# Three regroupings in a two-layer transformer kernel: the start's order, the last groups' output products, and where the quantiser runs

## The chip, the cores and the metric

The kernel runs on one core of one Trainium2 chip. Its time is the device time of one execution in microseconds (us), and the figure compared is the median over several executions. Below, the engines have the names of the profile: PE is the tensor engine (matrix products), DVE the vector engine, ACT the scalar engine, POOL the GpSimd engine, and SP the engine whose queue issues most of the DMA transfers. ACT also issues a few. Each engine works off its own instructions strictly in order.

## The reference

Input is x, 8 sequences of 512 tokens with 256 channels, in float32. Two layers follow each other, each of the form x + attention(norm(x)) + feed(norm(x)).

```python
xn = layernorm(x)
# layer 0
q, k, v = (xn @ W + b for W, b in ((Wq, bq), (Wk, bk), (Wv, bv)))   # 16 heads of 64
q, k = rope(q), rope(k)
p = softmax(where(causal, q @ k.T / sqrt(64), -1e9))
attention = (p @ v) @ Wo + bo
x_scale = max(abs(xn).max() / 127, 1e-5)          # over all 8 sequences
x_int8 = clip(round(xn / x_scale), -128, 127)
feed = (x_int8 @ weight_int8.T) * x_scale * weight_scale + bias
x = x + attention + feed
# layer 1
xn = layernorm(x)
comparison = (xn @ compare_left) @ (xn @ compare_right).T / sqrt(256)
attention = (comparison > threshold) * softmax(comparison + gate_bias) @ xn
prev = xn shifted down by one token, zeros first
r = sigmoid((mu_r * xn + (1 - mu_r) * prev) @ W_r.T)
k = square(relu((mu_k * xn + (1 - mu_k) * prev) @ W_k.T))
feed = r * (k @ W_v.T)
return x + attention + feed
```

## The kernel before

**Order.** Both layers are written under a manual schedule: the order of the calls in the source is the order of the instructions on every engine. Each call below (scores, soften, divide, ...) issues to one or several engines, so the place of a call decides what it stands behind on each of them. PSUM is eight banks of 128x512 float32, all of one pool (`bank`, L60); a bank comes free when its last reader has read it, and a product that finds no free bank waits.

**Layer 0** works in 16 groups `at`: sequence b = at // 2, and half g of its heads (8 heads). For each group:

- `project_qk` (L352), for half a group and for queries (0) or keys (1): eight products on PE (L363), two copies with bias on ACT into a buffer l (L368), and four DMAs on SP's queue that write l with its quarters swapped into y (L370). l and y have two buffers each. `turn_qk` (L373) applies the rotation: two products on DVE (L378), into h and in place in y, and the add h + y on POOL (L381).
- `project_v` (L384): products (L392), copies on ACT (L398), and a store to DRAM; `load_v` reads it back in another layout as vr.
- `scores(at, run)` (L418), in five runs, each with one or two pairs of banks sc (L429). `soften` (L436): DVE adds the mask and takes row minima (L452), ACT takes the exponential (L456) with its sum. `divide` (L462): reciprocals on DVE (L467), scaling on POOL (L472). `turn` (L480): transposes on DVE (L492).
- `weigh` (L497): 256 small products on PE (L505) into four banks av, when all five runs are turned. `keep_weighed` (L513): ACT copies them into four tiles att (L519).
- `finish` (L331), one group later: 16 products pw per half of the tokens with wo on PE (L340) and the sum with x1 on DVE (L344); after a sequence's second group x1 is stored to DRAM.

Around these: `look_at` and `prepare` normalise an input, `transpose_x` transposes it on PE, stores the transposed one in DRAM as xnf and keeps its greatest magnitude. When the last has been seen, `scale_of_x` makes the quantiser's scale xs. `quantise(b, r, xq)` (L177) then takes the tile read back from xnf (128x1024, float32, xnl) in three steps on POOL to whole numbers kept in bf16:

```python
nc.gpsimd.tensor_scalar(r, r, xs[:, 1:2], ROUND, ALU.mult, ALU.add)      # L181
nc.gpsimd.tensor_scalar(xq_, r, -ROUND, -128.0, ALU.add, ALU.max)        # L182
nc.gpsimd.tensor_scalar(xq_, xq_, 127.0, 127.0, ALU.min, ALU.min)        # L183
```

`add_quantised` (L185) multiplies xq with the int8 weights held in bf16 (PE, L191), scales on DVE (L196) and adds to x1 on POOL (L199). Sequences 0 and 1 are done inside groups 12 and 13, between `project(at + 1, 0)` and `scores(at, 2)`; sequences 2 to 7 in layer 1.

The head of the layer (L530 to L562), where the pipeline fills, and its tail (L647 to L682, groups 14 and 15) are written out by hand. Weights come by `load_group(which, g, n)`: which is 0 for q, 1 for k, 2 for v, and a quarter g is one tile of 4 heads. `load_rest` and `load_second` issue wo and other constants on ACT's queue.

**Layer 1** is one loop over b (L829 to L856): `compare` (c L727, row maxima L731, exponentials L740, threshold L743), `key` (pk L755, relu on ACT L759, square on POOL L760), `turn_input(b + 1)` (pyt L215), `gate` (pg L770, sigmoid L774), `sides_of(b + 1)` (plr L226), `mix` (ACT L706, DVE L710), `value` twice (pvv L782, product on DVE L786, sum on POOL L787), `turn_chances` (trc L795, copies ptc on ACT L797 and DVE L799), `complete` (the quantised part of sequence b + 2), `end` twice (po L808, y L814, store), `norm(b + 2)`, and `fetch_late(b + 3)`, which fetches x1 and xnf of that sequence and quantises it.

Of the kernel before, what the change touches and what calls it, by code (L numbers as in the profile page):

```python
# [16 lines left out]
P = 128  # L17
# [27 lines left out]
def two_layers(  # L45
# [131 lines left out]
    def quantise(b, r, xq):  # L177

        r = r.rearrange("p a n -> p (a n)")
        xq_ = xq.rearrange("p k n -> p (k n)")  # L180
        nc.gpsimd.tensor_scalar(r, r, xs[:, 1:2], ROUND, ALU.mult, ALU.add)  # L181
        nc.gpsimd.tensor_scalar(xq_, r, -ROUND, -128.0, ALU.add, ALU.max)  # L182
        nc.gpsimd.tensor_scalar(xq_, xq_, 127.0, 127.0, ALU.min, ALU.min)  # L183
# [57 lines left out]
    with ExitStack() as c0:  # L241
# [9 lines left out]
        away = pool("away", 2, space=bass.MemoryType.DRAM)  # L251

# [70 lines left out]
        def fetch(b):  # L323
            x1s[b] = output_tile(f"x1_{b}")
            nc.sync.dma_start(x1s[b], tokens(b))
# [5 lines left out]
        def finish(at):  # L331

            b, g = divmod(at, NH)
            for half in range(2):
                rows = slice(2 * half, 2 * half + 2)
                pw = bank(f"pw_{at}_{half}").rearrange("p (j n) -> p j n", j=2)
                for j in range(2):
                    tok = bass.ts(2 * half + j, P)
                    for p in range(4):
                        nc.tensor.matmul(  # L340
                            pw[:, j, :], atts[at, p][:, tok], wo[:, 4 * g + p, :],
                            start=(p == 0), stop=(p == 3),
                        )
                nc.vector.tensor_tensor(x1s[b][:, rows, :], pw, x1s[b][:, rows, :], ALU.add)  # L344
            if g == NH - 1:
                nc.sync.dma_start(x1_far[b], x1s[b].rearrange("p t n -> p (t n)"))

# [165 lines left out]
        def keep_weighed(at):  # L513
            g = at % NH
            for j, av in enumerate(weighed.pop(at)):
                atts[at, j] = attp.tile([P, S], F32, tag="att", name=f"att_{at}_{j}")
# [16 lines left out]
        project_qk(0, 0)  # L533
        project_qk(0, 1)
        turn_qk(0, 0)
        project_qk(1, 0)
        turn_qk(0, 1)
        x_next.append(load_x(1))
        project_qk(1, 1)
        for which in (1, 0, 2):  # L540
            load_group(which, 2, 2)
        turn_qk(1, 0)
        project_v(0)
        turn_qk(1, 1)
# [12 lines left out]
        turn_qk(2, 0)  # L557
        project_qk(3, 0)
        scores(0, 1)
# [3 lines left out]
        for at in range(last):  # L563
# [67 lines left out]
            soften(at, 4)  # L631
            turn(at, 3)
            if two:
# [10 lines left out]
            elif at == last - 1:  # L644
                nc.sync.dma_start(w2, second.rearrange("j (k p) n -> p j k n", p=P))
# [28 lines left out]
        finish(at - 1)  # L674
# [10 lines left out]
    with ExitStack() as c1:  # L685
# [7 lines left out]
        def fetch_late(b):  # L693
            fetch_output(b, act.tile([P, NT, D], F32, tag="x1", name=f"x1l_{b}", bufs=4))
            xq = act.tile([P, NK, S], BF16, tag="xq", name=f"xq_{b}")
            quantise(b, fetch_input(b, act.tile([P, NK, S], F32, tag="xnl", name=f"xnl_{b}")), xq)
            return xq
# [130 lines left out]
        xq = fetch_late(2)  # L828
        for b in range(B):  # L829
            compare(b)  # L830
            kk = key(b)
            if b + 1 < B:
# [19 lines left out]
            if b + 3 < B:  # L852
                xq = fetch_late(b + 3)
# [69 lines left out]
```

## Time and profile before

| quantity | value |
|---|---|
| times of 3 runs | 991.24, 994.87, 997.51 us; median 994.87 |
| profiled execution, its own time | 990.11 us |
| span of the profile | 988.0 us |
| mean granted PE clock in it | 0.986 of full |
| PE busy | 942.1 us, 95% |
| DVE busy | 777.1 us, 79% |
| POOL busy | 599.5 us, 61% |
| ACT busy | 530.2 us, 54% |
| DMA | 106.45 MB, mean 108 GB/s |

The span is the time between the first and the last recorded instruction; the execution's own time is 2.1 us longer. A row of a group list reads: line, engine, operation, output<-input with sizes, number of instructions, then busy us and mean ns of one, then the engine's idle time just before these instructions and what ended it. A row of a timeline reads: start in us, duration in us, engine, line, operation, and in brackets the idle time before it with its releaser. "issue" as releaser means that the profile shows nothing that was waited for. A q after an engine's name (ACTq) is its queue of DMA issues.

### The profile page before, as it was taken

Reading aid. Unit: us, or ns where it says so; the run is one execution under the profiler, and the core shown is the slowest. Engines: PE = TensorE matmul, PEld = TensorE weight load, DVE = VectorE, ACT = ScalarE, POOL = GpSimd, SP = SyncE. Lnnn points to the kernel's source line nnn. Section 1 sums busy time; section 2 is a strip of 40 time slices with the busy share of each in tenths; the row PEclk is TensorE's granted clock in tenths of the full one; section 3 lists DMA queues with packets and bytes.
Section 4 is the critical chain, followed back from the end, with each engine's and each line's share of the span. In section 5 each row is a group of like instructions: output and inputs, shape, how many; then the busy total and the mean of one; then the engine's idle time right before and its main releaser. Section 6 shows DMA issues by size and latency. Waiting matters only on the chain.

```text
span 988.0 us, 27412 instructions
## 1 busy us (share of the span) xinstructions
PE 942.1 (95%) x10491; PEld 599.9 (61%) x10491; DVE 777.1 (79%) x2417; ACT 530.2 (54%) x1480; POOL 599.5 (61%) x710
## 2 busy tenths in 40 slices
PE   9898999999999999999999999999797799999998
PEld 5345565655657565656566565656376576667776
DVE  4597988898899889887988997889876477677764
ACT  3365565656564755655575647474653534445553
POOL 3396665656575666666555758897644356566621
PEclk9899999999999999999999999999898999999999
DMA  6784354525452553445255445443530212221110
GB/s 186 198 238 108 87 123 138 127 70 132 143 127 69 132 143 91 109 150 117 78 130 150 123 116 130 132 127 73 132 88 13 75 64 75 76 75 52 45 32 33
DMA packets 61219, 106.45 MB, mean 108 GB/s; under 512 B 7585, under 2 KB 38305, under 8 KB 61089
## 3 DMA queue, kind: packets, MB, share of 16 engines
q1 hardware_dynamic: 59216, 103.06, 38.4%
q8 instruction: 83, 1.36, 0.6%
q10 hardware_dynamic: 1872, 1.64, 0.5%
q14 instruction: 48, 0.39, 0.1%
HBM read 39.66 MB, written 29.36 MB: 70 GB/s over the span
## 4 chain that ended last, share of the span: by engine, by line
PE 80%; POOL 8%; DVE 4%; issue 4%; DMA 3%; ACT 1%; SPq 0%; DVEq 0%; ACTq 0%; POOLq 0%
PE pq L363 21%; PE av L505 13%; PE sc L429 13%; PE pw L340 11%; PE pv L392 10%; PE po L808 3%; PE pvv L782 3%; POOL xq L182 2%; POOL xq L183 2%; PE trc L795 1%; POOL kk L760 1%; DMA xnl<-xnf 1%; DVE p L452 1%; PE pk L755 1%; PE acc L191 1%
## 5 line engine op out<-in xcount | busy, mean ns | idle before, releaser
L456 ACT ACTIVATE p<-p,nm 128x64 f32<-128x64 f32 (+15 forms) x512 | 260.0, 511 | 152.9 <-DVE nm L452 122.3
L472 POOL TENSOR_SCALAR p<-p,rs 128x64 f32<-128x64 f32 (+15 forms) x512 | 264.6, 542 | 55.0 <-DVE rs L467 53.6
L381 POOL TENSOR_TENSOR h<-h,y 128x1024 f32<-128x1024 f32 x64 | 167.8, 2622 | 189.2 <-DVE y L378 100.6
L452 DVE CUSTOM_DVE_ANT_0 p<-sc,cmask 128x64 f32<-128x64 f32 (+15 forms) x512 | 191.0, 436 | 77.1 <-PE sc L429 76.6
L492 DVE STREAM_TRANSPOSE t<-p 128x256 f32<-128x256 f32 (+3 forms) x640 | 193.5, 368 | 22.3 <-POOL p L472 20.0
L429 PE MATMUL sc<-h,h 64*32 64x512 f32 (+15 forms) x4096 | 145.9, 397 | 7.6 <-POOL h L381 6.0
L505 PE MATMUL av<-t,vr 32*64 32x96 f32 (+15 forms) x4096 | 131.6, 400 | 13.4 <-issue 13.4
L505 PEld LDWEIGHTS av<-t,vr 32*64 32x64 f32 x4096 | 126.2, 133 | 18.7 <-issue 15.8
L429 PEld LDWEIGHTS sc<-h,h 64*32 64x32 f32 x4096 | 76.9, 106 | 93.2 <-issue 66.9
L363 PE MATMUL pq<-xnT,wk 128*128 128x512 f32 x256 | 116.9, 609 | 6.1 <-DMA wk<-in_Wk 4.6
L368 ACT ACTIVATE l<-pq,cs 128x512 f32<-128x512 f32 x128 | 84.4, 682 | 67.5 <-PE pq L363 58.2
L378 DVE TENSOR_TENSOR y<-y,cs 128x1024 f32<-128x1024 f32 x64 | 109.4, 1710 | 8.7 <-DMA y<-l 8.7
L340 PE MATMUL pw<-wo,att 128*128 128x256 f32 x512 | 114.5, 381 | 0.7 <-ACT att L519 0.7
L363 PE MATMUL pq<-xnT,wq 128*128 128x512 f32 x256 | 114.4, 598 | 0.2 <-ACT xnT L299 0.2
L392 PE MATMUL pv<-wv,xnT 128*128 128x512 f32 x256 | 114.0, 598 | 0.0
L340 PEld LDWEIGHTS pw<-wo,att 128*128 128x128 f32 x512 | 95.7, 190 | 16.6 <-issue 2.1
L456 ACT ACTIVATION_READ_ACCUMULATOR p<-p,nm 128x1 f32 x512 | 96.9, 189 | 0.0
L363 PEld LDWEIGHTS pq<-xnT,wk 128*128 128x128 f32 x256 | 48.3, 194 | 67.9 <-issue 63.7
L392 PEld LDWEIGHTS pv<-wv,xnT 128*128 128x128 f32 x256 | 47.4, 190 | 57.7 <-issue 54.2
L519 ACT ACTIVATE att<-av,cs 128x512 f32<-128x512 f32 x64 | 38.9, 688 | 80.8 <-PE av L505 80.8
L378 DVE TENSOR_TENSOR h<-l,cs 128x1024 f32<-128x1024 f32 x64 | 78.8, 1231 | 4.3 <-ACT l L368 4.3
L363 PEld LDWEIGHTS pq<-xnT,wq 128*128 128x128 f32 x256 | 47.4, 190 | 56.6 <-issue 48.3
(95 smaller groups left out, 1005.9 us busy)
## 6 DMA issues: line engine op xcount, KB each, us to landing
y<-l SPq DMA_DIRECT2D x256, 128.0 KB, 2.3
va<-v SPq DMA_DIRECT2D x32, 512.0 KB, 3.0
vr<-va SPq DMA_DIRECT2D x64, 256.0 KB, 4.6
x<-in_x SPq DMA_DIRECT2D x15, 512.0 KB, 4.4
xnf<-xnT SPq DMA_DIRECT2D x8, 512.0 KB, 3.9
x1f<-x SPq DMA_DIRECT2D x8, 512.0 KB, 2.8
xnl<-xnf SPq DMA_DIRECT2D x8, 512.0 KB, 5.0
out<-y SPq DMA_DIRECT2D x14, 256.0 KB, 2.7
```

The costliest lines, as they stand in the source:

```text
L340: nc.tensor.matmul(pw[:, j, :], atts[at, p][:, tok], wo[:, 4 * g + p, :], start=(p == 0), stop=(p == 3),)
L363: nc.tensor.matmul(pb, w[:, g, k, bass.ts(t, P)], xnT[b][:, k, :], start=(k == 0), stop=(k == NK - 1),)
L368: nc.scalar.activation(l[:, t, :], pb, AF.Identity, bias=cs[:, bias : bias + 1])
L378: nc.vector.tensor_tensor(dst, src, table[:, None, :].to_broadcast([P, 2, S]), ALU.mult)
L381: nc.gpsimd.tensor_tensor(h, h, y, ALU.add)
L392: nc.tensor.matmul(pb.rearrange("p (g n) -> p g n", g=2), xnT[b][:, k, bass.ts(2 * half + j, P)], wqkv[2][:, 2 * g : 2 * g + 2, k, :], sta ...
L429: nc.tensor.matmul(scored[at, i][e][j * Q : j * Q + Q, :], q[rows, j % 2, bass.ts(i, Q)], k[rows, j % 2, :n], start=True, stop=True,)
L452: nc.vector.tensor_tensor_reduce(p[:, e, col : col + n], sc, cmask[:, S - n :], -1.0 / L**0.5, BIG, ALU.add, ALU.min, nm[:, c : c + 1],)
L456: nc.scalar.activation(p[:, e, col : col + n], p[:, e, col : col + n], AF.Exp, bias=nm[:, c : c + 1], scale=-1.0, accum_out=sm[:, c : c + 1],)
L472: nc.gpsimd.tensor_scalar(p, p, rs[:, c : c + 1], 1.0, ALU.mult, ALU.mult)
L492: nc.vector.transpose(turned[at][c][:, :, at_ : at_ + (n - 1) * pitch(c) + 1 : pitch(c), :], p[:, :, c * P : c * P + n * Q].rearrange("p e ...
L505: nc.tensor.matmul(banks[j][e * L : e * L + L, i * Q :], vs[at][rows, m, c, bass.ts(e, L)], t[c][rows, e, m * pitch(c) + m : m * pitch(c) ...
```

## The change

It has three parts.

1. **Start.** The loads of the second halves of the weights are taken out of one loop and spread between the first `project_qk` calls; the projections of group 2's keys and queries (`project_qk(2, 1)`, `project_qk(2, 0)`) are issued ahead of `project_v(0)`; the `turn_qk` calls and `divide(0, 0)` move with them. `load_group(2, 0, 2)`, which the top of the kernel issues too, appears a second time.
2. **Last groups.** `finish` is split into `output_product` (PE, one half) and `add_output` (DVE and the store). In groups 14 and 15 the products of group 13 stand between runs 2, 3 and 4 of group 15, those of group 14 after run 4 and `turn_input`, and the sums of both after the last `turn` (group 14's after `weigh(15)`). `scores(15, 0)` is issued in iteration 14, `turn(14, 4)` after `scores(15, 1)`, the statistics of `norm(1)` ahead of run 2. x1 of the last sequence and the four att tiles of group 14 get their place in buffers of y and l that are no longer used (`spare`).
3. **Quantiser.** The second step stays on POOL but works in place in float32, the minimum with 127 is a DVE instruction that writes bf16. In layer 1 `quantise(b + 2)` is issued behind `key(b)`, and `fetch_late(b + 3)`, which now only fetches, right after it.

```diff
         nc.gpsimd.tensor_scalar(r, r, xs[:, 1:2], ROUND, ALU.mult, ALU.add)
-        nc.gpsimd.tensor_scalar(xq_, r, -ROUND, -128.0, ALU.add, ALU.max)
-        nc.gpsimd.tensor_scalar(xq_, xq_, 127.0, 127.0, ALU.min, ALU.min)
+        nc.gpsimd.tensor_scalar(r, r, -ROUND, -128.0, ALU.add, ALU.max)
+        nc.vector.tensor_scalar(xq_, r, 127.0, None, ALU.min)
...
+        def spare(tag, n):
+            return work.tile([P, 2, S], F32, tag=tag, name=f"spare_{tag}_{n}", bufs=2)
...
-        def finish(at):
+        output = {}
+        def output_product(at, half):
+            g = at % NH
+            pw = bank(f"pw_{at}_{half}").rearrange("p (j n) -> p j n", j=2)
+            for j in range(2):
...
+                    nc.tensor.matmul(
+                        pw[:, j, :], atts[at, p][:, tok], wo[:, 4 * g + p, :],
+                        start=(p == 0), stop=(p == 3),
+                    )
+            output[at, half] = pw
+        def add_output(at):
             b, g = divmod(at, NH)
             for half in range(2):
                 rows = slice(2 * half, 2 * half + 2)
+                nc.vector.tensor_tensor(
+                    x1s[b][:, rows, :], output.pop((at, half)), x1s[b][:, rows, :], ALU.add
+                )
             if g == NH - 1:
                 nc.sync.dma_start(x1_far[b], x1s[b].rearrange("p t n -> p (t n)"))
+        def finish(at):
+            output_product(at, 0)
+            output_product(at, 1)
+            add_output(at)
...
         project_qk(0, 0)
+        load_group(1, 2, 2)
         project_qk(0, 1)
         turn_qk(0, 0)
+        load_group(0, 2, 2)
         project_qk(1, 0)
         turn_qk(0, 1)
+        load_group(2, 0, 2)
+        project_qk(1, 1)
+        turn_qk(1, 0)
         x_next.append(load_x(1))
-        project_qk(1, 1)
-        for which in (1, 0, 2):
-            load_group(which, 2, 2)
-        turn_qk(1, 0)
+        project_qk(2, 1)
+        turn_qk(1, 1)
+        load_group(2, 2, 2)
+        project_qk(2, 0)
+        look_at(1)
+        turn_qk(2, 1)
         project_v(0)
-        turn_qk(1, 1)
-        look_at(1)
         prepare(1)
-        project_qk(2, 1)
-        project_qk(2, 0)
+        turn_qk(2, 0)
         scores(0, 0)
         soften(0, 0)
-        turn_qk(2, 1)
-        divide(0, 0)
         project_qk(3, 1)
         load_v(0)
         load_rest()
         load_second()
-        turn_qk(2, 0)
         project_qk(3, 0)
+        divide(0, 0)
         scores(0, 1)
...
             scores(at, 4)
             soften(at, 4)
+            if at == last - 1:
+                nc.sync.dma_start(w2, second.rearrange("j (k p) n -> p j k n", p=P))
+                fetch(B - 1, spare("y", 0).rearrange("p k (t n) -> p (k t) n", n=D))
+                scores(last, 0)
             turn(at, 3)
+            if at == last - 1:
+                break
...
         at = last
-        scores(at, 0)
         soften(at, 0)
-        finish(at - 2)
-        fetch(B - 1)
+        divide(at - 1, 4)
+        scores(at, 1)
         turn(at - 1, 4)
-        scores(at, 1)
-        divide(at, 0)
         soften(at, 1)
         weigh(at - 1)
-        keep_weighed(at - 1)
+        keep_weighed(at - 1, [l[:, t, :] for l in (spare("l", n) for n in range(2)) for t in range(2)])
         load_v(at)
+        divide(at, 0)
+        normalise_1 = norm(1, xpool.tile([P, NT, D], F32, tag="x", name="yn_1"))
+        scores(at, 2)
+        output_product(at - 2, 0)
         divide(at, 1)
-        scores(at, 2)
-        turn_input(0, whole("yt_0", S + 1))
+        normalise_1()
         turn(at, 0)
         soften(at, 2)
+        add_biases(B - 1)
         turn(at, 1)
         scores(at, 3)
+        output_product(at - 2, 1)
         divide(at, 2)
-        add_biases(B - 1)
         soften(at, 3)
         scores(at, 4)
         turn(at, 2)
         soften(at, 4)
         divide(at, 3)
-        finish(at - 1)
+        turn_input(0, whole("yt_0", S + 1))
+        output_product(at - 1, 0)
+        output_product(at - 1, 1)
         turn(at, 3)
         divide(at, 4)
         sides_of(0, first_sides[:, 0, :], first_sides[:, 1, :])
         turn(at, 4)
+        add_output(at - 2)
         weigh(at)
         keep_weighed(at)
-        norm(1, xpool.tile([P, NT, D], F32, tag="x", name="yn_1"))()
+        add_output(at - 1)
         finish(at)
...
             compare(b)
             kk = key(b)
+            if b + 2 < B:
+                xq = act.tile([P, NK, S], BF16, tag="xq", name=f"xq_{b + 2}")
+                quantise(b + 2, xnl, xq)
+            if b + 3 < B:
+                xnl = fetch_late(b + 3)
             if b + 1 < B:
                 turn_input(b + 1, act.tile([P, NK, S + 1], F32, tag="xt", name=f"yt_{b + 1}"))
...
-            if b + 3 < B:
-                xq = fetch_late(b + 3)
             end(b, (2,), pt, r, y)
```

More of the change, by code (lines that the diff above doesn't have):

```diff
@@ L321, in two_layers, with fetch @@
         atts = {}
-        def fetch(b):
-            x1s[b] = output_tile(f"x1_{b}")
+        def fetch(b, dst=None):
+            x1s[b] = dst if dst is not None else output_tile(f"x1_{b}")
             nc.sync.dma_start(x1s[b], tokens(b))
@@ L329, in add_biases @@
                 nc.gpsimd.tensor_tensor(x1s[b][:, t, :], x1s[b][:, t, :], bob, ALU.add)
-        def finish(at):
+        output = {}
[3 more added lines that the diff above has]
+            for j in range(2):
+                tok = bass.ts(2 * half + j, P)
+                for p in range(4):
+                    nc.tensor.matmul(
[4 more added lines that the diff above has]
+        def add_output(at):
             b, g = divmod(at, NH)
@@ L335, in finish @@
                 rows = slice(2 * half, 2 * half + 2)
[L336 to L344, printed above, removed]
+                nc.vector.tensor_tensor(
+                    x1s[b][:, rows, :], output.pop((at, half)), x1s[b][:, rows, :], ALU.add
+                )
             if g == NH - 1:
                 nc.sync.dma_start(x1_far[b], x1s[b].rearrange("p t n -> p (t n)"))
+        def finish(at):
+            output_product(at, 0)
+            output_product(at, 1)
+            add_output(at)
         heads_of, vs = {}, {}
@@ L511, in weigh, with keep_weighed @@
             weighed[at] = banks
-        def keep_weighed(at):
+        def keep_weighed(at, dst=None):
             g = at % NH
             for j, av in enumerate(weighed.pop(at)):
-                atts[at, j] = attp.tile([P, S], F32, tag="att", name=f"att_{at}_{j}")
+                atts[at, j] = dst[j] if dst else attp.tile([P, S], F32, tag="att", name=f"att_{at}_{j}")
                 bv = BIAS + 2 * NP + 4 * g + j
@@ L643, in two_layers @@
                 greatest()
-            elif at == last - 1:
-                nc.sync.dma_start(w2, second.rearrange("j (k p) n -> p j k n", p=P))
         at = last
-        scores(at, 0)
         soften(at, 0)
-        finish(at - 2)
-        fetch(B - 1)
+        divide(at - 1, 4)
+        scores(at, 1)
         turn(at - 1, 4)
-        scores(at, 1)
-        divide(at, 0)
         soften(at, 1)
         weigh(at - 1)
-        keep_weighed(at - 1)
+        keep_weighed(at - 1, [l[:, t, :] for l in (spare("l", n) for n in range(2)) for t in range(2)])
         load_v(at)
+        divide(at, 0)
+        normalise_1 = norm(1, xpool.tile([P, NT, D], F32, tag="x", name="yn_1"))
+        scores(at, 2)
+        output_product(at - 2, 0)
         divide(at, 1)
-        scores(at, 2)
-        turn_input(0, whole("yt_0", S + 1))
+        normalise_1()
         turn(at, 0)
         soften(at, 2)
+        add_biases(B - 1)
         turn(at, 1)
         scores(at, 3)
+        output_product(at - 2, 1)
         divide(at, 2)
-        add_biases(B - 1)
         soften(at, 3)
@@ L694, in fetch_late @@
             fetch_output(b, act.tile([P, NT, D], F32, tag="x1", name=f"x1l_{b}", bufs=4))
-            xq = act.tile([P, NK, S], BF16, tag="xq", name=f"xq_{b}")
-            quantise(b, fetch_input(b, act.tile([P, NK, S], F32, tag="xnl", name=f"xnl_{b}")), xq)
-            return xq
+            return fetch_input(b, act.tile([P, NK, S], F32, tag="xnl", name=f"xnl_{b}"))
         def complete(b, xq):
@@ L827, in two_layers @@
         mix(0, 0)
-        xq = fetch_late(2)
+        xnl = fetch_late(2)
         for b in range(B):
```

## The prediction, made before the changed kernel was run

> **What bounds the kernel now.** First the busy shares: TensorE (PE) 942.1 of a span of 988.0 us, VectorE (DVE) 79%, GpSimd (POOL) 61%. So a gain must be one of PE's 42 us of gaps and slow stretches, and a loss must open a new gap. The chain that ended last says who stands in them, and the waits of PE name the lines:
>
> ```profile
> PE 80%; POOL 8%; DVE 4%; issue 4%; DMA 3%; ACT 1%; SPq 0%; DVEq 0%; ACTq 0%; POOLq 0%
> ```
>
> ```profile
> PE av L505 <- issue: 13.4, 5, 6.1
> PE pvv L782 <- POOL kk L760: 10.1, 11, 3.7
> PE sc L429 <- POOL h L381: 6.0, 2, 5.6
> PE pq L363 <- DMA wk<-in_Wk: 4.6, 1, 4.6
> ```
>
> The columns are total us, number of waits, longest. The PE timeline puts them in place. Between 84 and 592 there is almost none: PE is busy 506.7 of 509 us. They lie at the start, in the tail of the attention (groups 14 and 15) and in the second layer, where the change works:
>
> ```profile
> 33.91 6.12 PE L363 MATMUL pq<-xnT,wk 128*128 128x512 f32 x8 [4.62 <-DMA wk<-in_Wk]
> 83.02 2.00 PE L505 MATMUL av<-t,vr 32*64 32x512 f32 x11 [4.19 <-issue]
> 714.65 3.61 PE L429 MATMUL sc<-h,h 64*32 64x512 f32 x40 [5.57 <-POOL h L381]
> 755.87 9.44 PE L505 MATMUL av<-t,vr 32*64 32x512 f32 x256 [6.07 <-issue]
> 790.14 5.28 PE L782 MATMUL pvv<-wk,kk 128*128 128x256 f32 x16 [3.72 <-POOL kk L760]
> ```
>
> Columns: start, duration, instruction, and in brackets PE's idle time before it. The gap at 678.67, 0.96 before av(13), also counts below. PE is in order, so all of 4.62, 4.19, 5.57, 6.07 and 3.72 is time that only an earlier releaser gives back.
>
> **Part 1, the start.** The loads of wk[2:4] and wq[2:4] go from 28.74 and 29.36 on SP's queue, behind the four y DMAs of two projections, to about 15.5 and 18.7, and group 2's projections stand before the first values. The 4.62 goes, and so does the slow start after it: L363 took 6.12+3.60 there against 3.70+3.60 (45.28, 48.82). That is 7.0 us of PE, but PE isn't what ends the stage: av(0) at 83.02 waits for DVE's last transpose, and what fed DVE is ScalarE's queue:
>
> ```profile
> 49.02 0.43 ACTq L266 DMA_DIRECT2D wo<-in_Wo  x1
> 54.89 0.36 ACTq L135 DMA_DIRECT2D gs<-in_gates  x1
> 55.45 1.27 ACT L368 ACTIVATE l<-pq,cs 128x512 f32<-128x512 f32 x2 [5.50 <-DMA rw<-in_rows]
> ```
>
> ACT issues the load of wo, then the issue of gs waits until about the 1 MB of wo has landed, and the projection's copy and every exponential of scores(0,1) stand behind it. The change keeps these loads behind project_qk(3,1). I place soften(0,0) at 42.4 instead of 44.6, and the exponentials of run 1 at 55.0 instead of 56.6, since h_2_0 is ready only at about 44.9 (two y buffers, each free after a GpSimd add) and wo then shares the DMA engines with y and vr. From there to 83 DVE has hardly a gap. So av(0) moves with the exponentials: **-1.5 us**. Ends: -4 if the wait for wo shrinks, -0.5 if the second load of wv (512 KB, now issued twice) delays y.
>
> **Part 2, the quantiser, eight tiles.** Removed on POOL: L182 and L183. Added: the same add/max in place in float32 on POOL, and one minimum on DVE that writes bf16.
>
> ```profile
> L182 POOL TENSOR_SCALAR xq<-xnl 128x1024 bf16<-128x1024 f32 x8 | 29.1, 3641 | 0.7
> L183 POOL TENSOR_SCALAR xq<-xq 128x1024 bf16<-128x1024 bf16 x8 | 29.1, 3638 | 0.7
> L181 POOL TENSOR_SCALAR xnl<-xnl,xs 128x1024 f32<-128x1024 f32 x8 | 9.0, 1123 | 36.3 <-DMA xnl<-xnf 36.3
> ```
>
> The new second step isn't in the trace. Ends: 1.12 (L181, same tile, float32) and 3.64 (L182, same operation, bf16 out). I take 1.12: L182 holds one maximum and L183 two minimums, yet both take 3.64, and what they share apart from L181 is the bf16 side. The Trainium skill ("GPSIMD Engine Reference", section "4.1 Engine selection") speaks against the idea that much is to be won: a one-input operation on GpSimd runs at about line rate, and it knows no dtype in this. By that rule all three steps would cost 1.1, and the change saves 1.1 us of POOL a tile; by the rows 3.64+3.64-1.12 = 6.16. The rows decide. The minimum on DVE: 0.8 by the cast of w8b (0.40 for half the columns) to 1.22 by L378; I take 1.1.
>
> The skill also says ("SBUF — State Buffer", section "Who interferes with whom") that GpSimd and some VectorE operations, tensor_scalar among them, lock each other out of a shared port pair. The trace shows such a thing: eight L472 took 3.65 alone and 5.6 to 5.7 beside a two-input L378. By the rule the minimum could hold up a GpSimd operation for its 1.1, or wait for one, up to 2.4 (an L381 add). But after its second step POOL has nothing ready: the next operation is a gate add or an h add that waits for DVE itself. I put nothing; the other end is +1 a tile.
>
> *Groups 12 and 13.* The minimum stands in DVE's queue before soften(at,2), behind two POOL steps that stand behind divide(at,1):
>
> ```profile
> 601.14 3.65 POOL L472 TENSOR_SCALAR p<-p,rs 128x448 f32<-128x448 f32 x8 [2.34 <-DVE rs L467]
> 604.76 1.13 POOL L181 TENSOR_SCALAR xnl<-xnl,xs 128x1024 f32<-128x1024 f32 x1
> ```
>
> ```profile
> 604.52 0.56 DVE L452 CUSTOM_DVE_ANT_0 p<-sc,cmask 128x384 f32<-128x384 f32 x1 [3.42 <-PE sc L429]
> ```
>
> So 604.76+1.13+1.12 = 607.0, and with the minimum soften(12,2) starts at about 608 instead of 604.5; in group 13 at about 655.6 instead of 651.4. Behind it in DVE's queue: the masks that free score banks, turn_qk's products, the transposes. In group 12 DVE's next idle stretch (1.01 at 613.5) and PE's queue take up most; the output product of group 11 needs a score bank and waits some 1.2. In group 13 the delay reaches turn(13,4): 679.9 becomes 681.8, and av(13)'s gap of 0.96 becomes 3.0. POOL's relief of 6.2 us a group lies beside PE here. **+3.2**, ends 0 and +5.
>
> *Second layer.* The squares of kk now stand ahead of the quantiser on POOL, and its input is fetched an iteration earlier.
>
> ```profile
> 834.99 1.12 POOL L181 TENSOR_SCALAR xnl<-xnl,xs 128x1024 f32<-128x1024 f32 x1 [2.90 <-DMA xnl<-xnf]
> 836.20 3.64 POOL L182 TENSOR_SCALAR xq<-xnl 128x1024 bf16<-128x1024 f32 x1
> 839.92 3.64 POOL L183 TENSOR_SCALAR xq<-xq 128x1024 bf16<-128x1024 bf16 x1
> 843.52 2.04 POOL L760 TENSOR_TENSOR kk<-kk 128x512 f32<-128x512 f32 x2
> ```
>
> ```profile
> 844.62 0.70 PE L782 MATMUL pvv<-wk,kk 128*128 128x256 f32 x2 [0.83 <-POOL kk L760]
> 845.61 3.29 PE L782 MATMUL pvv<-wk,kk 128*128 128x256 f32 x14 [0.30 <-POOL kk L760]
> ```
>
> POOL runs without a break from 835 to 845.5 and PE waits for its last step. Put kk first and it is ready at about 838. For b=0: pvv starts at 786.4 rather than 790.14 (-3.7), at its usual 3.6 rather than 5.28 (-1.7), and DVE's ptc copy, late by its mixes, gives 0.6 back: **-4.8**. For b=1 to 5: 0.83 to 1.21 before the first pvv and 0.30 inside, with the records around it 1.5 to 1.7, less about 0.5 that po then waits for DVE's ptc copy L799 (the minimum falls in DVE's 4.7 us hole before the mix at 845): 1.1 each, **-5.5**. Ends: -8.5 (all of 1.7), 0.
>
> **Part 3, the tail.** sc(15,0) still waits for the h add of the last query projection: DVE and POOL ahead of it are unchanged, so the 5.57 stays. The 7.17 us output product of group 13 that followed it on PE goes behind runs 2 and 3, so PE stands about 5.4 idle until turn(14,4) at 724.1, which before came 726.8 because DVE's sums of that product stood ahead of it. av(14) ends at 733.5 instead of 735.2. After that it is DVE's and POOL's softmax chain: the sums L344 (1.26 and 1.3) move behind turn(15,4), the statistics of norm(1) (2.9) move in, and the last transpose ends at 755.0 instead of 756.1. The 6.07 of waiting is filled with products, so av(15) runs at 7.95, as elsewhere, and not at 9.44; one of its banks waits about 0.6 for add_output(13). End 763.6 instead of 765.3: **-1.7**. Ends -4 and +2 (norm(1) waits in DVE's queue for POOL's rstd). The fetch of x1l_2 now waits for the store of x1_7 (2.8 us); that is hidden, since the quantiser that reads the same iteration's fetches stands behind the kk squares at 784.
>
> **Sum** against the profiled execution's 990.11: -1.5 +3.2 -4.8 -5.5 -1.7 = -10.3. That execution lay 0.5% under the median of the three runs, 994.87; the difference carries over: **984.6**.
>
> **Rivals.**
> - *The operation, not bf16, is slow* (chance 0.12): the second step stays 3.64. Groups 12 and 13 then hold DVE 2.5 us longer each: +8.2. In the second layer kk is still first, but the quantiser ends late, b=0 gains 1.5 and b=1 to 5 lose 0.9 each: +3. With -1.5 and -1.7: **1002.9**, slower than before. It decides from a second step above about 2.5 us. For it: max and min are what L182 and L183 have and L181 hasn't. Against: one and two of them cost the same.
> - *DVE becomes the second layer's bound* (0.18): the minimum, the mixes and the ptc copies take up the 5.5 of b=1 to 5, so the sum is -10.3+5.5 = -4.8: **990.1**. For it: DVE is nearly closed from 845 to 858 in an iteration. Against: its 4.70 hole before.
> - *Little comes back* (0.14): groups 12 and 13 swallow their delay and the second layer gains its 1.7 an iteration: -1.5+0-4.8-8.5-1.7 = -16.5: **978.4**.
> - The forecast, 0.56; its own range is 979 to 991.
>
> **Numbers.** About 1% is what a measurement of this kernel tells from no change: 984.9 and 1004.8. The forecast's case lies about evenly on both sides of the first, 0.29 and 0.27; the little-comes-back case gives 0.13 to faster; DVE's case gives 0.03 to faster and 0.15 to the same; the slow quantiser is half and half. Faster 0.45, same 0.48, slower 0.07. The range 974 to 997 leaves out the slow quantiser and the far low end.
>
> **What would show it.** Right: a new L182 at 1.1 us with float32 out; kk squares before L181 in the second layer; no gap before pvv; no gap at 29; gaps of about 1 and 3 in groups 12 and 13; a 5 us gap before av(14) and none before av(15). Wrong: L182 at 3.6; a po that waits for DVE by more than 1 us an iteration; an av(0) before 79 or after 83; av(15) ending after 765.

## The result: slower, because GpSimd's second step kept its 3.64 us

Six runs of the changed kernel took 999.57 to 1003.62 us, median 1001.55. Six of the kernel before on the same chip had a median of 994.69. The ratio is 1.0065, with a 95% interval of 1.0039 to 1.0091. That is slower by 0.65%, inside the 1% band, but outside the predicted range of 974 to 997, and on the other side of no change. It lies 1.4 us from the first rival's 1002.9. The four signs of being wrong that the prediction listed were all there: L182 at 3.64, a po that waits 1.29 for DVE, av(0) at 85.12 and av(15) ending at 776.1.

The profiled execution of the changed kernel is a typical one (1001.49, span 999.4). That of the kernel before, 990.11, lay 4.6 under its median of 994.69. So the two traces stand 11.4 us apart where the medians stand 6.9 apart. The table splits the 11.3 us between the ends of the last products on PE, each stage measured from the end of the one before.

| stage on PE | before | changed | difference | predicted |
|---|---|---|---|---|
| to the end of av(11) | 592.23 | 594.17 | +1.9 | -1.5 |
| av(11) end to av(13) end (groups 12, 13) | 95.45 | 107.21 | +11.8 | +3.2 |
| av(13) end to av(15) end (tail) | 77.63 | 74.75 | -2.9 | -1.7 |
| av(15) end to po(0) end | 39.64 | 40.10 | +0.5 | -4.8 |
| po(0) end to po(5) end | 134.16 | 134.20 | 0.0 | -5.5 |
| po(5) end to po(7) end | 45.04 | 45.04 | 0.0 | 0 |

Waiting is the smaller part of the 11.3. PE stood idle for 48.9 us of its span instead of 45.9, but the same 10491 products kept it busy for 950.5 us instead of 942.1. They took longer where the profile shows a lower granted clock, in stretches behind some of the waits. At the start, where the transposes on DVE decide, that need not cost time. In groups 12 and 13, where it matters most, PE's idle time rose from 2.4 to 8.8 and its busy time from 93.0 to 98.4, at a mean granted clock of 0.95 instead of 1.00.

First the groups of POOL and DVE by line and shape (busy us, mean ns; then idle before and its releaser):

```profile
L182 POOL TENSOR_SCALAR xnl<-xnl 128x1024 f32<-128x1024 f32 x8 | 29.1, 3636 | 0.7
L183 DVE TENSOR_SCALAR xq<-xnl 128x1024 bf16<-128x1024 f32 x8 | 5.5, 694 | 54.5 <-POOL xnl L182 54.5
```

Float32 changed nothing in L182: 3636 ns against 3641. The minimum on DVE is cheap, 0.69, but DVE stood 54.5 us idle in front of eight of them. Then the waits of PE:

```profile
PE av L522 <- issue: 11.3, 5, 4.2
PE po L833 <- DVE ptc L824: 7.1, 6, 1.3
PE sc L446 <- POOL h L398: 6.0, 2, 5.6
...
PE pk L780 <- issue: 3.4, 1, 3.4
```

The wait of pvv for kk and the wait of pq for wk are gone, as forecast. In their place stand two that were not there: po for the ptc copy on DVE, and a single wait of pk.

**Groups 12 and 13**, the timelines of DVE, POOL and PE in the changed kernel, and last av(13) in the kernel before:

```profile
603.67 0.20 DVE L484 RECIPROCAL rs<-sm 128x4 f32<-128x4 f32 x2
612.40 0.69 DVE L183 TENSOR_SCALAR xq<-xnl 128x1024 bf16<-128x1024 f32 x1 [8.53 <-POOL xnl L182]
```

```profile
603.90 3.63 POOL L489 TENSOR_SCALAR p<-p,rs 128x448 f32<-128x448 f32 x8 [3.06 <-DVE rs L484]
607.51 1.12 POOL L181 TENSOR_SCALAR xnl<-xnl,xs 128x1024 f32<-128x1024 f32 x1
608.72 3.65 POOL L182 TENSOR_SCALAR xnl<-xnl 128x1024 f32<-128x1024 f32 x1
```

```profile
622.22 7.14 PE L344 MATMUL pw<-wo,att 128*128 128x256 f32 x32 [1.96 <-DVE nm L469]
...
690.58 10.80 PE L522 MATMUL av<-t,vr 32*64 32x512 f32 x256 [3.27 <-issue]
```

```profile
679.63 8.05 PE L505 MATMUL av<-t,vr 32*64 32x512 f32 x256 [0.96 <-issue]
```

DVE handed POOL its reciprocals at 603.9 and did nothing until POOL had scaled (3.63), multiplied (1.12) and clamped (3.65). Everything behind the minimum in DVE's queue came late. PE first missed a bank that a mask had not yet freed (1.96), then the transposes of group 13, the last of which DVE began at 690.03 (3.27). And av(13) took 10.80 at a granted clock of 0.73, where before it had taken 8.05 at 1.00.

Some 2.0 us of the 11.8 stand ahead of the moved minimum and are not its work. The first scores and query products of group 12 took 2.96 and 7.83 at a granted clock of 0.84, behind a wait of 1.55, against 2.10, 7.13 and 1.15 before. The run b_start below, which leaves these groups as they were, shows the same in its trace (2.95 and 7.93 at 0.84, behind 2.23).

**The second layer.** One iteration, b = 2, on PE, then what stands behind the minimum on DVE and ACT:

```profile
859.72 1.04 PE L191 MATMUL acc<-w8b,xq 128*128 128x256 bf16 x8
861.20 1.99 PE L833 MATMUL po<-yn,ptc 128*128 128x256 f32 x8 [0.44 <-ACT ptc L822]
864.48 5.45 PE L833 MATMUL po<-yn,ptc 128*128 128x256 f32 x24 [1.29 <-DVE ptc L824]
```

```profile
857.30 0.69 DVE L183 TENSOR_SCALAR xq<-xnl 128x1024 bf16<-128x1024 f32 x1 [6.22 <-POOL xnl L182]
857.94 0.06 DVE L211 MEMSET yt<- 128x2 f32 x1
...
863.75 1.27 DVE L824 COPY ptc<-trc 128x512 f32<-128x512 f32 x2
```

```profile
858.11 2.56 ACT L731 ACTIVATE mix<-yt,nmus 128x512 f32<-128x512 f32 x4 [2.81 <-DVE yt L211]
860.58 1.04 ACT L822 COPY ptc<-trc 128x512 f32<-128x512 f32 x2
```

Before the change PE waited in this iteration for kk (0.83 and 0.30 before pvv) and for the threshold e (0.27 before pg). These waits are gone, but 0.44 and 1.29 before po stand in their place, and an iteration takes 26.8 us as before. DVE reaches its mixes and its ptc copy late, because the minimum in front of them waits for L182. ACT's mixes and copies are late for the same reason: they wait for the memset of yt, which stands behind the minimum on DVE.

### The profile page after: what moved, and what is told of

Read it like the earlier page. It is cut to its first block, busy times and chain, and to the rows that moved or that the text cites. A ratio compares the mean times of both kernels' runs of the same rounds, so it can differ in the third digit from the quotient of the medians.

```text
span 999.4 us, 27419 instructions
## 1 busy us (share of the span) xinstructions
PE 950.5 (95%) x10491; PEld 605.7 (61%) x10491; DVE 776.8 (78%) x2425; ACT 528.4 (53%) x1480; POOL 568.9 (57%) x702
## 3 DMA queue, kind: packets, MB, share of 16 engines
q1 hardware_dynamic: 59360, 103.59, 38.2%
## 5 line engine op out<-in xcount | busy, mean ns | idle before, releaser
L446 PE MATMUL sc<-h,h 64*32 64x512 f32 (+15 forms) x4096 | 152.1, 408 | 11.4 <-POOL h L398 6.0
L522 PE MATMUL av<-t,vr 32*64 32x96 f32 (+15 forms) x4096 | 134.8, 407 | 11.3 <-issue 11.3
L446 PEld LDWEIGHTS sc<-h,h 64*32 64x32 f32 x4096 | 80.8, 109 | 99.0 <-issue 68.3
L380 PE MATMUL pq<-xnT,wk 128*128 128x512 f32 x256 | 114.2, 598 | 1.3 <-ACT xnT L303 1.3
L395 DVE TENSOR_TENSOR y<-y,cs 128x1024 f32<-128x1024 f32 x64 | 107.3, 1677 | 10.4 <-DMA y<-l 10.3
L344 PE MATMUL pw<-wo,att 128*128 128x256 f32 x480 | 107.8, 382 | 2.7 <-DVE nm L469 2.0
L344 PEld LDWEIGHTS pw<-wo,att 128*128 128x128 f32 x480 | 89.7, 190 | 18.2 <-issue 4.7
L536 ACT ACTIVATE att<-av,cs 128x512 f32<-128x512 f32 x60 | 36.3, 688 | 72.3 <-PE av L522 72.3
```

Source lines behind the costliest of these rows:

```text
L344: nc.tensor.matmul(pw[:, j, :], atts[at, p][:, tok], wo[:, 4 * g + p, :], start=(p == 0), stop=(p == 3),)
L380: nc.tensor.matmul(pb, w[:, g, k, bass.ts(t, P)], xnT[b][:, k, :], start=(k == 0), stop=(k == NK - 1),)
L395: nc.vector.tensor_tensor(dst, src, table[:, None, :].to_broadcast([P, 2, S]), ALU.mult)
L446: nc.tensor.matmul(scored[at, i][e][j * Q : j * Q + Q, :], q[rows, j % 2, bass.ts(i, Q)], k[rows, j % 2, :n], start=True, stop=True,)
L522: nc.tensor.matmul(banks[j][e * L : e * L + L, i * Q :], vs[at][rows, m, c, bass.ts(e, L)], t[c][rows, e, m * pitch(c) + m : m * pitch(c) ...
```

## The experiments

All ratios are to runs of the kernel before on the same chip as the experiment. The chips differ by half a per cent (medians of the kernel before: 993.2, 999.0 and 998.6), so ratios are compared, not times. In the table the columns are stages of each run's one trace, cut as above; the one headed c(0) to pk(0) is the time from the start of c(0), the second layer's first comparison, to the start of pk(0), its first key product. The kernel before appears twice in groups 12 and 13, since b_start leaves them as they were: 95.45 and 98.55. Differences under 3 us in that column, and under 2.4 in the last (134.16 and 136.50), are no result by themselves.

| kernel | ratio (95% interval) | groups 12, 13 | c(0) to pk(0) | po(0) to po(5) |
|---|---|---|---|---|
| before | 1 | 95.45 | 1.92 | 134.16 |
| changed | 1.0065 (1.0039 to 1.0091) | 107.21 | 5.39 | 134.20 |
| b_quant | 1.0096 (1.0061 to 1.0131) | 109.09 | 1.92 | 134.18 |
| b_start | 0.9989 (0.9971 to 1.0006) | 98.55 | 1.92 | 136.50 |
| a_fastq | 1.0082 (1.0053 to 1.0112) | 106.20 | 5.38 | 134.29 |
| a_latemin | 1.0146 (1.0106 to 1.0187) | 114.51 | 5.38 | 134.25 |
| a_midmin | 0.9967 (0.9952 to 0.9983) | 101.14 | 5.38 | 134.28 |
| a_x17 | 0.9995 (0.9980 to 1.0010) | 105.75 | 1.95 | 134.25 |
| a_loads | 1.0026 (1.0011 to 1.0042) | 109.86 | 5.39 | 134.21 |
| a_fma | 0.9864 (0.9838 to 0.9890) | 102.10 | 5.39 | 122.89 |
| a_best | 0.9767 (0.9744 to 0.9790) | 96.04 | 1.95 | 122.89 |
| a_best2 | 0.9732 (0.9716 to 0.9747) | 97.88 | 1.95 | 122.89 |

### What makes the second step slow: rows, a_fastq, rows2

The first thought was that a maximum or a minimum costs. rows gave each sequence of the second layer another form of the step. Like rows2 below it computes something else than the reference and was run once; only the durations of this one step are used:

```diff
-        nc.gpsimd.tensor_scalar(r, r, -ROUND, -128.0, ALU.add, ALU.max)
...
+            3: (-ROUND, 0.0, ALU.add, ALU.add, F32), 4: (-ROUND, 0.0, ALU.add, ALU.add, BF16),
+            5: (127.0, 1.0, ALU.min, ALU.mult, F32), 6: (1.0, -128.0, ALU.mult, ALU.max, F32),
+            7: (127.0, None, ALU.min, None, F32),
+        }.get(b, (-ROUND, -128.0, ALU.add, ALU.max, F32))
```

> The changed kernel, but GpSimd's second quantiser step takes another form in each sequence of the second layer: sequence 2 add and maximum in float32 as changed; 3 add and add in float32; 4 add and add with bf16 output (and no minimum on VectorE); 5 minimum and multiply in float32; 6 multiply and maximum in float32; 7 one minimum alone in float32. It leaves out the clamp or the subtraction in sequences 3 to 7, so only the durations count. Theory 'operation': a maximum or a minimum costs, whatever the type: 3.6 in sequences 2, 5 and 6, 1.1 in 3, and 1.1 to 1.5 in 4; 7 tells whether one slow operation alone makes the 3.6. Rival 'bf16 and maximum both cost': 4 at 3.6 too. Rival 'the place, not the operation' (what stands before it, or in-place writing): all six at 3.6.

The timeline of POOL, sequences 2 to 7 in order:

```profile
801.82 3.64 POOL L189 TENSOR_SCALAR xnl<-xnl 128x1024 f32<-128x1024 f32 x1
...
828.67 3.64 POOL L189 TENSOR_SCALAR xnl<-xnl 128x1024 f32<-128x1024 f32 x1
...
855.51 3.64 POOL L189 TENSOR_SCALAR xq<-xnl 128x1024 bf16<-128x1024 f32 x1
...
880.05 3.65 POOL L189 TENSOR_SCALAR xnl<-xnl 128x1024 f32<-128x1024 f32 x1
...
907.03 3.65 POOL L189 TENSOR_SCALAR xnl<-xnl 128x1024 f32<-128x1024 f32 x1
...
933.90 2.79 POOL L189 TENSOR_SCALAR xnl<-xnl 128x1024 f32<-128x1024 f32 x1
```

The theory fell: add and add, with no clamp at all, took 3.64 too, in float32 and into bf16. One operation alone took 2.79. What was left was L181, which multiplies and then adds.

a_fastq, planned together with rows, rests on the theory that fell:

```diff
-        nc.gpsimd.tensor_scalar(r, r, -ROUND, -128.0, ALU.add, ALU.max)
-        nc.vector.tensor_scalar(xq_, r, 127.0, None, ALU.min)
+        nc.gpsimd.tensor_scalar(r, r, -ROUND, 0.0, ALU.add, ALU.add)
+        nc.vector.tensor_scalar(xq_, r, -128.0, 127.0, ALU.max, ALU.min)
```

> The changed kernel with the maximum moved from GpSimd to VectorE's instruction, which then holds maximum and minimum; GpSimd's second step is add and add in float32. Theory 'operation': that step falls from 3.64 to about 1.1, as the prediction had assumed; groups 12 and 13 lose 3 to 5 instead of 11.7, and the second layer's iterations 1 to 5 gain about 1 each: together 11 to 14 less, 988 to 991. Rival 'VectorE's ptc copies and mixes bound the second layer anyway': the groups' part alone, 7 to 9 less, 993 to 995. Rival 'the duration does not depend on the operation': 1001.5.

Its L182 took 3641 ns and its ratio is that of the change, 1.0082: the last rival's case, a plain miss for the theory.

rows2 took other forms in the same place, to part the order of operations from the kind of scalar:

```diff
+            2: (1.0, -ROUND, ALU.mult, ALU.add, F32), 3: (sc, -ROUND, ALU.mult, ALU.add, F32),
+            4: (1.0, -ROUND, ALU.mult, ALU.add, BF16), 5: (sc, 0.0, ALU.add, ALU.add, F32),
+            6: (sc, 1.0, ALU.mult, ALU.mult, F32), 7: (2.0, 1.0, ALU.mult, ALU.mult, F32),
```

> The changed kernel with other forms of GpSimd's second quantiser step in the second layer's sequences: 2 multiply by a constant and add a constant, float32; 3 the same with the multiplier from a column of a tile; 4 multiply and add with constants, bf16 output (no minimum on VectorE); 5 add a column and add a constant; 6 multiply by a column and by a constant; 7 multiply by two constants. It leaves out the clamp and, in 5 to 7, the arithmetic, so only durations count. So far multiply-and-add (L181) took 1.12 and every form with an add first, a maximum or a minimum 2.8 to 3.65. Theory 'multiply-then-add is one fast routine': 2, 3 and perhaps 4 at 1.1, and 5 and 7 near 3.6; 6 near 2.1, since L472 of that form takes 1.115 for 512 columns. Rival 'the scalar's kind decides, a column is fast and a constant slow': 3, 5 and 6 at 1.1 to 2.2, and 2, 4 and 7 at 3.6.

```profile
799.50 1.05 POOL L189 TENSOR_SCALAR xnl<-xnl 128x1024 f32<-128x1024 f32 x1
...
825.41 1.12 POOL L189 TENSOR_SCALAR xnl<-xnl,xs 128x1024 f32<-128x1024 f32 x1
...
849.99 1.05 POOL L189 TENSOR_SCALAR xq<-xnl 128x1024 bf16<-128x1024 f32 x1
...
874.57 3.72 POOL L189 TENSOR_SCALAR xnl<-xnl,xs 128x1024 f32<-128x1024 f32 x1
...
901.51 1.13 POOL L189 TENSOR_SCALAR xnl<-xnl,xs 128x1024 f32<-128x1024 f32 x1
...
926.03 1.05 POOL L189 TENSOR_SCALAR xnl<-xnl 128x1024 f32<-128x1024 f32 x1
```

Multiply and add is fast (1.05 with a constant, 1.12 with a column), also into bf16, and multiply and multiply as well. Add and add is slow with a column too. So neither type nor the scalar's kind decides, and the theory's 3.6 for two constant multiplications and 2.1 for a column and a constant were wrong as well. Of the forms tried, a multiplication followed by a multiplication or an addition is fast and every other is slow. Why is not shown.

### The price that the prediction assumed: a_fma

```diff
-        nc.gpsimd.tensor_scalar(r, r, -ROUND, -128.0, ALU.add, ALU.max)
-        nc.vector.tensor_scalar(xq_, r, 127.0, None, ALU.min)
+        nc.gpsimd.tensor_scalar(r, r, 1.0, -ROUND, ALU.mult, ALU.add)
+        nc.vector.tensor_scalar(xq_, r, -128.0, 127.0, ALU.max, ALU.min)
```

> The changed kernel with GpSimd's second step as multiply by 1.0 and add -ROUND in float32 (1.05 to 1.12 in the run of forms), and maximum and minimum in VectorE's one instruction. This is the price that the prediction had assumed, with all else as in the change. Theory 'the wrong duration is what failed in groups 12, 13 and in the second layer': between av(11) and av(13) 5 to 7 less than the changed kernel's 106 to 107, in the second layer's iterations 1 to 5 about 8 less than its 134.2 us, the 3.4 before pk(0) stays: 13 to 15 less, ratio to before 0.991 to 0.994. Rival 'the minimum's place alone makes the loss, whatever the step takes': at most 3 less between av(11) and av(13).

```profile
L182 POOL TENSOR_SCALAR xnl<-xnl 128x1024 f32<-128x1024 f32 x8 | 8.4, 1044 | 0.7
```

Ratio 0.9864. With this one duration at 1.04 instead of 3.64 the change is faster by 1.4%: times 994.87 that is 981.3, where the prediction had 984.6. The gain is larger than expected (0.991 to 0.994). Groups 12 and 13 fell by 5.1 against the changed kernel, iterations 1 to 5 by 11.3. The PE timeline of an iteration has no wait left in it:

```profile
845.49 3.62 PE L807 MATMUL pvv<-wk,kk 128*128 128x256 f32 x16
848.94 1.91 PE L820 MATMUL trc<-ident,e 128*128 128x128 f32 x16
850.68 1.04 PE L191 MATMUL acc<-w8b,xq 128*128 128x256 bf16 x8
851.56 7.07 PE L833 MATMUL po<-yn,ptc 128*128 128x256 f32 x32
```

### The third part alone: b_quant

The kernel before with the diff's changes to `quantise`, `fetch_late` and the second layer's loop, and nothing else.

> The kernel before with the third part of the change alone: the quantiser's second step in float32 on GpSimd, the minimum on VectorE, and the second layer's new order. Theory 'the minimum in VectorE's queue costs': groups 12 and 13 lose about 9 to 11 us between the end of av(11) and the end of av(13), the second layer's first product pk(0) keeps its place behind c(0) (no 3.4 gap) and pvv(0) comes about 3 earlier, iterations 1 to 5 come out even; together +6 to +8, 1001 to 1003, ratio 1.006 to 1.008. Rival 'the loss in groups 12 and 13 needs the new tail or the new start': under 4 us there and a time of at most 996.

Groups 12 and 13 took 109.09, 10.5 to 13.6 over the two traces of the kernel before: the loss needs neither the new start nor the new tail. pk(0) keeps its place, and po(0) ends 3.06 earlier relative to it; iterations 1 to 5 come out even. The ratio, 1.0096, is a little above what was expected.

### The place of the minimum: a_latemin, a_midmin

Both leave L182 at 3.64 and move only DVE's instruction in groups 12 and 13. First a_latemin:

```diff
             if at in (last - 3, last - 2):
+                nc.vector.tensor_scalar(xq..., xnl..., 127.0, None, ALU.min)
                 for half in range(2):
                     add_quantised(s_, half, xq, line(f"u_{s_}_{half}"))
```

> The changed kernel with one instruction moved: in groups 12 and 13 the minimum on VectorE stands after divide(at,3), ahead of the int8 products, instead of ahead of soften(at,2). GpSimd's 3.6 us step stays. Theory 'VectorE waits in its queue': the 8.5 us idle stretches of VectorE ahead of the minimum go, and the 11.7 us that these groups lose fall to 2 at most: 991 to 993. Rival 'GpSimd's own time is what is late': VectorE's idle time moves to another wait for GpSimd, less than 4 us come back: 998 or more.

It was slower, 1.0146. VectorE's 8.5 us stretch is gone, as the theory says, but now the minimum came too late for PE:

```profile
623.74 1.89 PE L193 MATMUL acc<-w8b,xq 128*128 128x256 bf16 x8 [6.78 <-DVE xq L645]
```

The same wait had only been moved to the engine that sets the time. a_midmin puts it behind turn_qk(2*at+2,0), ahead of turn(at,1):

> The changed kernel with one instruction moved: in groups 12 and 13 the minimum on VectorE stands behind turn_qk(2*at+2,0), ahead of turn(at,1), so that masks of run 2 and the rotation stand before it and the int8 products' input is still in time. Expected after the run with the minimum ahead of the int8 products, where VectorE's stretch of 8.5 us went but PE waited 6.8 for the minimum itself. Theory 'each queue waits for what stands in front in it': no stretch of VectorE before the minimum over 1 us, no wait of PE before the int8 products, and the 11.7 us lost between av(11) and av(13) fall to 1 or less: about 990 to 992. Rival 'GpSimd's time is what is late': 5 or more stay lost there.

Ratio 0.9967, against 1.0065 of the changed kernel: the same work on the same engines, one instruction in another place. 6.1 of the 11.8 came back in the trace, not all: 3.2 of them idle time and 2.9 faster products, as the mean granted clock there was 0.97 instead of 0.95. DVE and POOL in group 13 show one reason:

```profile
660.30 2.84 DVE L627 TENSOR_SCALAR xq<-xnl 128x1024 bf16<-128x1024 f32 x1 [0.41 <-POOL xnl L182]
```

```profile
660.24 2.35 POOL L400 TENSOR_TENSOR h<-h,y 128x1024 f32<-128x1024 f32 x1
```

The minimum takes 0.69 elsewhere. Here it began just after a GpSimd add and ended 0.55 after it. That is how the lock of a shared port, which the prediction weighed and put at nothing, would look: about 2.1 for one tile, twice its other end.

### The gap before pk(0): a_x17

```diff
-                fetch(B - 1, spare("y", 0).rearrange("p k (t n) -> p (k t) n", n=D))
+                fetch(B - 1, wqkv[2].rearrange("p g k n -> p (g k n)")[:, : NT * D].rearrange("p (t n) -> p t n", n=D))
```

> The changed kernel with the last sequence's x1 in the memory of the value weights, which belongs to the outer pool, instead of in a y buffer of the first layer's pool. Theory 'the second layer's first tile waits for the last use of every tile of the closed pools, and the store of that x1 is one': ACT's first mix starts right after the last output product, the 3.4 us gap of PE before pk(0) goes, 3 less in all: 998 to 999. Rival 'the memory of one tile is what it waits for' (a tile of the second layer lies on the y buffer): the same gap goes only if that tile is the mix's own, and it is not; the gap stays, 1001.5.

ACT in the changed kernel, then in a_x17:

```profile
788.08 2.56 ACT L731 ACTIVATE mix<-yt,nmus 128x512 f32<-128x512 f32 x4 [9.53 <-DMA x1f<-spare_y]
```

```profile
783.83 2.56 ACT L731 ACTIVATE mix<-yt,nmus 128x512 f32<-128x512 f32 x4 [6.09 <-issue]
```

The gap before pk(0) went, so it was the store of this x1 out of that y buffer that held the mix. Whether the mix waits for the last use of every tile of the first layer's pools, as the theory has it, or for the memory of this one buffer stays open, since no run shows where the tiles lie. The ratio, 0.9995, is 7 us under the changed kernel's. That is more than the 3.4 us gap. In this trace av(13) also took 8.05 rather than 10.80 behind the same 3.27 wait, at a granted clock of 1.00 rather than 0.73, so 2.7 of it need not come from the edit.

### The start: b_start, a_loads

b_start is the kernel before with the start's new order and loads.

> The kernel before with the first part of the change alone: the start's new order and loads. The prediction gave this part -1.5. Theory 'av(0) hangs on the exponentials behind the load of wo, and these are not earlier, since VectorE's queue holds the second input's statistics and normalising ahead of the first masks': -0.5 to +1.5 at av(0), ratio 0.999 to 1.002. The prediction's step: ratio 0.9985 or less. Rival 'the second load of the value weights costs': av(0) 2 later and more, ratio over 1.002.

Ratio 0.9989, interval 0.9971 to 1.0006: the prediction's -1.5 us (0.9985) lies in it, and so does no change. In its trace av(0) starts at 83.74, against 83.02 before. The +1.9 of the first row of the stage table is no result by itself either: with this start, av(11) ends between 591.43 here and 595.15 in a_x17.

a_loads issues wo last on ACT's queue, in the changed kernel:

```diff
-                (wo, Wo.rearrange("(c p) n -> p c n", p=P)),
                 (rest[0], w8.rearrange("(k p) n -> p k n", p=P)),
                 (rw, rows.to_broadcast([P, 3 * D]).rearrange("p (r n) -> p r n", r=3)),
+                (wo, Wo.rearrange("(c p) n -> p c n", p=P)),
...
+        load_second()
         load_rest()
-        load_second()
```

> The changed kernel with one thing moved in the start: wo, the largest of the loads on ACT's queue, is issued last of them, after gs. Theory 'the exponentials of scores(0,1) wait for wo through the issue of gs': ACT's wait of 5.4 before the projection's copy goes, these exponentials start at about 54 instead of 58.8, and av(0) starts 2 to 4 earlier than the 83.8 to 85.1 of the changed kernel, at 80 to 82; ratio 1.002 to 1.005. Rival 'VectorE or GpSimd end the start's stage anyway': ACT's wait goes, av(0) stays within 1.

ACT in the changed kernel, then in a_loads:

```profile
57.65 1.26 ACT L385 ACTIVATE l<-pq,cs 128x512 f32<-128x512 f32 x2 [5.35 <-DMA y<-l]
58.80 0.67 ACT L473 ACTIVATE p<-p,nm 128x448 f32<-128x448 f32 x1
```

```profile
54.65 1.26 ACT L385 ACTIVATE l<-pq,cs 128x512 f32<-128x512 f32 x2 [0.95 <-ACT l L385]
55.81 0.66 ACT L473 ACTIVATE p<-p,nm 128x448 f32<-128x448 f32 x1
```

ACT's wait of 5.35 fell to 0.95 and the exponentials of run 1 started at 55.81 instead of 58.80, yet av(0) started at 85.35. That is the rival's case: DVE and POOL end the stage. The trace does not part the two cleanly, though: its soften(0,0) began at 48.34 instead of 46.93, and from there to av(0) it took 37.0 instead of 38.2, so some 1.2 was gained. The ratio, 1.0026, lies in the band that was given for the other case, 3.9 us under the changed kernel's, and the trace shows only that 1.2. How much the wait for wo costs stays open.

### Putting it together: a_best, a_best2

a_best is the changed kernel with the multiply-and-add step, the x1 of a_x17, and in groups 12 and 13 the DVE instruction directly behind soften(at,2). a_best2 also issues wo last and drops the second load of the value weights.

```diff
             scores(at, 2)
             soften(at, 2)
+            if at in (last - 3, last - 2):
+                nc.vector.tensor_scalar(xq..., xnl..., -128.0, 127.0, ALU.max, ALU.min)
```

> The changed kernel with three repairs: the fast second step (multiply and add), the VectorE instruction of groups 12 and 13 behind soften(at,2) instead of ahead of it, where GpSimd has nothing running beside it, and the last x1 in the value weights' memory. By the runs so far: about 9 to 10 less between av(11) and av(13) (to 97), 3.4 less before pk(0), 8 to 9 less in iterations 1 to 5 of the second layer: 20 to 22 under the changed kernel, ratio to before 0.983 to 0.987. If the effects do not add (VectorE or GpSimd ends the second layer's iteration anyway): 0.99 or more.

> The same with wo issued last on ACT's queue, and without the second load of the first value weights. If the start's stage hangs on the wait for wo: another 2 to 4 less, ratio 0.980 to 0.984; if on VectorE and GpSimd: equal to the version without it within 1 us.

a_best has a ratio of 0.9767, better than the 0.983 to 0.987 expected, and a_best2 one of 0.9732, 4.2 us less. Both beat both kernels: their medians are 975.52 and 971.29, against 998.58 for the kernel before. In a_best2's trace soften(0,0) begins at 44.9 instead of 46.7, and av(0) at 81.74, also 1.75 before a_best's: it is the earlier second input that shows, which points to the dropped load rather than to wo. The two edits were not tried apart. Its waits of PE are what a next change would look at:

```profile
PE av L524 <- issue: 8.4, 4, 3.6
PE sc L448 <- POOL h L400: 5.6, 1, 5.6
```

## Why the prediction was wrong, point by point

- **The failing step: "I take 1.12: L182 holds one maximum and L183 two minimums, yet both take 3.64, and what they share apart from L181 is the bf16 side."** They share something else: neither is a multiplication followed by a multiplication or an addition. The nearest row was chosen by shape and type, and neither decided. The step measured 3.64. With the price of 1.12 nearly made true (1.04 in a_fma), the kernel came out at 0.9864, so this term carries the failure. The prediction's own first rival, at a chance of 0.12, had the step at 3.64 and the kernel at 1002.9, though its reason (maximum and minimum) fell too in rows. That its sum lies so close is in part luck: it had +8.2 for groups 12 and 13 and +3 for the second layer, where the traces show +11.8 and +0.5. The line rate that the Trainium skill gives for one-input operations ("GPSIMD Engine Reference", section "4.1 Engine selection") does not name the form either; one-input steps measured from 1.05 to 3.72.
- **Groups 12 and 13: +3.2 predicted, +11.8.** The place was right: the minimum held DVE, PE missed a bank before a product of group 11 (1.2 forecast, 1.96 measured) and then the transposes of group 13 (3.0 forecast, 3.27). The start of the masks was forecast at 608 and came at 613.0, of which 2.5 is L182 and the other part the later arrival of the whole group. With L182 at 1.04, a_fma still took 102.10, 3.6 to 6.7 over the kernel before, so +3.2 was at the low side. The prediction counted the waits here and nothing for slower products behind them; in a_fma av(13) took 9.64 instead of 8.05 behind a wait of 2.54, at a granted clock of 0.82. The minimum itself, taken at 1.1, cost 0.69.
- **Second layer, b = 0: -4.8 predicted, +0.5.** Two terms. The quantiser behind kk gave -3.0 with L182 at 3.64, and -5.0 in a_fma (24.40 from pk(0) to the end of po(0), against 29.44), so this term was sized right. The store of the last x1, called hidden, cost 3.5 before pk(0). The step looked at x1l_2 alone, and not at the second layer's first mix, which waited for that store too. With both repaired, in a_best, the stage took 34.16, which is 5.5 less than before.
- **Iterations 1 to 5: -5.5 predicted, 0.0.** "DVE becomes the second layer's bound" was the right rival for these, with the mechanism named, but for the reason of L182 again. With the fast step the gain is 11.3, more than the -8.5 given as the end. The ceiling of 1.7 an iteration was mis-sized, since the iteration shrank by 2.25. It left out a wait in front of pg, which went too (b = 2):

```profile
838.35 3.72 PE L770 MATMUL pg<-wk,mix 128*128 128x256 f32 x16 [0.27 <-DVE e L743]
```

  And the records of instructions that follow without a wait overlap by some 0.16, so a wait shown as 0.83 costs about 1.0.
- **The tail: -1.7 predicted, -2.9.** Largely as forecast: the 5.57 before sc(15,0) stayed, a gap stood before av(14) (2.44 rather than about 5) and none before av(15), which ran at 7.91. No run tried the tail alone, but the stage took 77.63 to 79.55 in the three traces with the old tail and 74.49 to 75.19 in all with the new one.
- **The start: -1.5 predicted.** b_start's ratio gives -1.1, with an interval from -2.9 to +0.6, but the step "soften(0,0) at 42.4" was wrong; it came at 46.9. DVE's timeline of the changed kernel shows what stood ahead of it:

```profile
36.02 1.40 DVE L151 BATCH_NORM_STATS2 st_a<-x 128x6 f32<-128x256 f32 x4 [1.76 <-DMA x<-in_x]
...
40.09 3.40 DVE L161 TENSOR_SCALAR x<-x,mv_a,rstd_a 128x256 f32<-128x256 f32 x4
```

  The second input was issued at 31.2 and landed at 36.0, and its statistics and normalising stand in DVE's queue ahead of the masks. The working moved only PE's and ACT's instructions.
- **A slip without effect.** PE's gaps before the change are 988.0 - 942.1 = 45.9 us, not 42.

## What to carry to other kernels

Before an elementwise step on GpSimd is priced from a neighbouring row, compare the two operations in it, not only shape and type: here multiply-and-add took 1.05 and add-and-add 3.64 on the same tile, and rewriting x - c as 1.0*x - c was worth about 2% of the kernel (ratio 1.0082 in a_fastq, 0.9864 in a_fma). When one step of a chain is handed to another engine, ask where it stands in that engine's queue: the same instruction cost 8.7 to 11.8 us ahead of the masks and 2.6 to 5.7 behind them (by the two traces of the kernel before), and cost PE directly when it was put too late. When a buffer is borrowed near the end of a stage, ask whether the next stage's first instruction will wait for its last use: here a store out of it cost 3.5 us. And a ledger of waits alone falls short where the granted clock drops behind them: here PE's busy time rose by more than its idle time.

## What was not expected of the hardware

- GpSimd's tensor_scalar on 128x1024: 1.05 to 1.13 for multiply-add and multiply-multiply, 3.64 to 3.72 for add-add, add-maximum, multiply-maximum and minimum-multiply, 2.79 for a minimum alone; float32 and bf16 outputs alike.
- A DVE tensor_scalar of 0.69 took 2.84 when a GpSimd add had just begun, and four normalising instructions of 1.38 together took 3.40 where they ran beside GpSimd's h add of 2.45 (40.25 to 42.69).
- The same wait of 3.27 before av(13) was followed by 8.05 in two traces (a_fastq, a_x17; granted clock 1.00 in both) and by 10.66 to 10.90 in five others (0.72 to 0.74). Shorter waits go both ways too: behind 1.55 the next products of the changed kernel ran at 0.84, behind 2.31 those of b_quant at 1.00. Whether PE slows behind such a gap differs between executions, and it is one part of the spread of these kernels' times.
